# A graph-attention layer on one core: statistics of h from the gathered rows, three q tiles made ahead, weight loads behind the last k|v store, degrees kept in a table

## The chip, the core and the metric

The kernel runs on one core of one Trainium2 chip. The core has five engines, each with an in-order queue of its own: TensorE (PE, matrix products and transposes), VectorE (DVE), ScalarE (ACT), GpSimd (POOL), and SyncE (SP, which here only issues transfers). ACT and POOL issue transfers too. An instruction at the head of a queue that waits holds everything behind it in that queue.

The metric is the device time of one execution in microseconds, the median of several runs. Before the change it is 1834.15 us.

## The reference

A graph-transformer layer over 4096 nodes with 512 features. Source rows x and target rows h are normalized, q is made of h, and k and v of x, with 8 heads of 64. Each target node attends only to the nodes that its row of the 4096 x 4096 adjacency matrix names (about 17 of 4096, itself among them). Then come an output projection, a residual, a second normalization, a feed-forward net of 2048, two more residuals and a last normalization.

```python
hs = layer_norm(h_source, ln1_scale, ln1_bias)      # h_source is x
ht = layer_norm(h_target, ln1_scale, ln1_bias)
q = (ht @ Wq + bq).reshape(T, H, HD) / jnp.sqrt(jnp.float32(HD))
k = (hs @ Wk + bk).reshape(S, H, HD)
v = (hs @ Wv + bv).reshape(S, H, HD)
logits = jnp.einsum('thd,shd->hts', q, k)
logits = jnp.where(edge_mask[None] != 0, logits, NEG)
probs = jax.nn.softmax(logits, axis=-1)
ctx = jnp.einsum('hts,shd->thd', probs, v).reshape(T, D)
ht = ht + ctx @ Wo + bo
ht = layer_norm(ht, ln2_scale, ln2_bias)
out = ht + jax.nn.gelu(ht @ W1) @ W2
x = _layernorm(x + out)
```

## The kernel before

The kernel never forms the full logits. It reads the adjacency matrix once, turns each row into a short list of edges, and gathers the k|v rows that a list names.

**Stage 1: k|v rows and lists.** `project` takes x in 16 pairs of 128-row tiles: it measures each row (`measure`, with `stats`, L697 and L698), scales it on ACT (L890), transposes it on PE (L904), multiplies by Wk and Wv (L929, `source`), copies the products from PSUM (L931, ACT) and stores 128 rows of k|v in the DRAM table `kvd` (L935, issued by ACT). Beside it `edges(i)` reads the adjacency rows of tile i in four quarters of 512 KB (L713, issued by SP). ACT forms the signs of a quarter and counts them (L728), DVE weights them by position and finds the largest of five segments (L733, L735), and a decoding step at the end of a tile (L742 to L759) writes up to 24 column numbers into a record. What may be left over goes to `rest_d` (L766, issued by SP). The buffer is `ring`, 20 slots of 4 KB a partition: slots 0 to 7 hold quarters of the first NA + FILL tiles, 8 to 11 rows of h, 12 to 16 rows of x. Later quarters use two `wide` slots (17 and 18). Three sign buffers lie in slot 19. In the attention the slots 0 to 16, later 0 to 19, hold gathered k|v rows.

**Statistics of h.** In stage 1 the kernel also loads all 32 tiles of h in order of their rows (`ask`, L795) and measures them (`moments`, L805). At the end of the list stage it makes 1/sigma and -mean/sigma for all of them at once and writes both into the records (L1407 to L1411).

**The sort.** The records of 16 tiles are ordered by degree (`sort`): DVE counts, PE sums by matrix products (L838, L846), and POOL scatters 16 x 128 records to their places in DRAM (L853). After that, tile i of the attention holds nodes of like degree, and TILES gives each tile's largest degree, 11 to 39. The first half (NA = 16 tiles) is sorted in stage 1, the second half during the attention, after `other_lists`.

**The attention.** For a tile, `prefetch` loads its sorted records (L979), and `front` makes q in steps: gather rows of h by the TGT column (POOL), a small DVE step L994, normalization on ACT (L995), transposes (L999), the product with Wq (L1008) and the finish on DVE (L1013). L994 changes no value; it ties the record to the latest k|v copy or logits (`latest`), so that the front isn't issued too early. `issue` starts the gathers of k|v rows (L966, one per edge column), in groups of S = 3 columns. For a group, DVE forms the products with q (L1217) and the sums by head (L1222), ACT the exponentials, DVE and ACT the weighted v rows (L1181, L1201), and PE adds them up by transposing into PSUM (L1189). `finish` divides by the sum, projects (L1112), adds the residual, normalizes, and hands h2T to the FFN. `feed` runs the FFN of a group of tiles (L1325, L1328, L1334), and `end` the last normalization and the indirect store of the output. At the end `verdict` checks degrees and sums; the degrees come back from DRAM by two loads (L1259).

**What sets the order.** `_weave` runs generators as streams: each yields a cost, and the stream with the lowest total goes on. Streams of stage 1 are `projections`, `prepare` (lists of the first half, sort, first fronts) and `fill` (FILL more lists); of the second stage the attention, the FFN, `other_lists` and `weights`. That is the order in which instructions are written. A scheduler then moves them, engine by engine, by its own estimates, as far as dependences allow. The loads of the second half of W1 and W2 (`weights`, L586 and L587) are issued by ACT into memory that stage 1 gives back.

Of the kernel before, what the change touches and what calls it, by code (L numbers as in the profile page):

```python
# [377 lines left out]
DEG, TGT, ROW, RST, E0 = 0, 1, 2, 3, 5  # L378
# [65 lines left out]
def adj_resnorm_kernel(  # L444
# [88 lines left out]
    with tc.tile_pool(name="keep", bufs=1) as keep:  # L533
        ident = keep.tile([P, P], F32, name="ident")
        make_identity(nc, ident)
        mhalf = keep.tile([P, NT], F32, name="mhalf")
# [10 lines left out]
        degs = keep.tile([P, NT, 1], I32, name="degs")  # L547
# [3 lines left out]
        with ExitStack() as late:  # L551
# [57 lines left out]
            def list_constants():  # L609
# [17 lines left out]
                for R, (i0, n) in zip(Rs, PARTS):  # L627
                    nc.gpsimd.memset(R, 0)
                    for c, base in ((TGT, i0 * P), (ROW, 0)):
                        nc.gpsimd.iota(R[:, :, c], pattern=[[P, n]], base=base,  # L630
                                       channel_multiplier=1)
# [69 lines left out]
            held, moms = [], list(range(NT))  # L701
            mvh = wp.tile([P, NT, 2], F32, name="mvh")
# [3 lines left out]
            FILL = 5  # L706
# [9 lines left out]
            def edges(i):  # L716
# [4 lines left out]
                for h in range(NQ):  # L721
# [12 lines left out]
                    for s, (w0, w1) in enumerate(SEGS):  # L734
                        nc.vector.max(cand[:, h * SQ + s, :], wd[:, w0:w1])  # L735
                    if h == 1:
                        keep_rest()
                    if h % 2 and moms:
                        moments(moms.pop(0))
                    yield 2.0  # L740
# [20 lines left out]
                yield 4.0  # L761
# [29 lines left out]

            asked = list(range(NT))

            def ask(i):
                nc.sync.dma_start(hrow(i), h_target[i * P:(i + 1) * P, :])  # L795

            def hrow(i):
                return ring[:, DEEP + i // 2 % 4, i % 2 * D:(i % 2 + 1) * D]

            def moments(i):  # L800

                while asked and len(asked) > NT - 4 - i:
                    ask(asked.pop(0))
                t = hrow(i)
                stats(ip, t, mvh[:, i, :], "n0")  # L805

            def sort(part):
# [44 lines left out]
                for i in range(n):  # L852
# [7 lines left out]
                    yield 1.3  # L860
# [3 lines left out]
            def project(order, t=None):  # L864
# [54 lines left out]
                def source(n, j):  # L919
                    g, hT = order[n], state[n][1]  # L920
                    if asked or moms:
                        kvr = sp.tile([P, 2 * D], F32, name="tq", bufs=3)
                    else:

                        kvr = ring[:, 8 + (n * G + j) % 3, :]
# [6 lines left out]
                    if n >= 14:  # L932
                        latest[:] = [kvr[:, 0:1]]
                    r0 = 1 + (g * G + j) * P
                    nc.scalar.dma_start(kvd[r0:r0 + P, :], kvr)  # L935
# [27 lines left out]
            recs, tqs, h2Ts, done, ready, latest = {}, {}, {}, set(), [], []  # L963
# [187 lines left out]
            def first_fronts():  # L1151
# [6 lines left out]
                while not latest:  # L1158
                    yield None
# [326 lines left out]
```

## Time and profile before

| | us |
|---|---|
| median of 3 runs | 1834.15 |
| lowest and highest | 1833.16, 1836.34 |
| span of the profiled execution | 1826.4 |
| lists of the first half done, sort begins (L813) | 195.4 |
| scatter of the first sort, first and last | 240.8 to 261.5 |
| first gather of k|v rows issued | 301.6 |
| first value products on PE (L1189) | 320.1 |
| second sort begins (L813) | 591.5 |

The page cuts the span into 40 slices of 45.7 us. A digit is the busy share in tenths:

```profile
PE   7989983698998989999998998999999999999997
DVE  6999855999999838786967998999888797988200
ACT  5767634487987637676767777778777676787311
POOL 1000143746566477657567778877574656763101
PEclk9999996698999999999998999999999999999999
DMA  9999958988896648767769978787776767674000
```

Slices 1 to 6 are stage 1, 7 and 8 the passage to the attention, and the rest attention and FFN side by side. "PEclk" is the granted TensorE clock; it falls to about 0.7 in slices 7 and 8, where PE has little to do. In a group line the columns are: source line, engine and operation, output and input, shapes, count, then busy us and mean ns of one, then idle time of the engine just before. An idle time with an arrow names what ended it.

### The profile page before, as it was taken

The page shows a single profiled execution, that of the slowest core. Times are in us where ns is not written, and L with a number is a line of the kernel's source. Part 1 is how long each engine was busy: PE and PEld are TensorE (multiplying, and loading weights), DVE is VectorE, ACT ScalarE, POOL GpSimd, SP SyncE. Part 2 cuts the span into 40 slices and gives each one's busy share as a digit, 9 for nine tenths or more (in the row PEclk, how much of TensorE's full clock was granted, in tenths as well). Part 3 has the DMA queues.
Part 4 walks back from the last instruction along what each step waited for, and adds up shares of the span by engine and source line. Part 5 has one row for each costly group of instructions (what it writes and reads, how often), then busy time and mean ns, then how long its engine had stood idle before and what let it go on. Part 6 is the DMA issues. An engine that isn't in the chain of part 4 may idle for free. (4 is left out here: it accounts for less than half of the span.)

```text
span 1826.4 us, 22937 instructions
## 1 busy us (share of the span) xinstructions
PE 1687.8 (92%) x7030; PEld 1102.5 (60%) x7030; DVE 1432.2 (78%) x2628; ACT 1222.0 (67%) x3119; POOL 973.8 (53%) x834
## 2 busy tenths in 40 slices
PE   7989983698998989999998998999999999999997
PEld 3444431475666656767676666666666666667664
DVE  6999855999999838786967998999888797988200
ACT  5767634487987637676767777778777676787311
POOL 1000143746566477657567778877574656763101
PEclk9999996698999999999998999999999999999999
DMA  9999958988896648767769978787776767674000
GB/s 354 373 395 365 341 192 309 360 291 312 286 331 231 209 121 312 245 239 260 261 211 308 308 245 302 252 296 265 240 272 222 256 214 262 228 269 159 17 7 25
DMA packets 144396, 463.27 MB, mean 254 GB/s; under 512 B 20628, under 2 KB 25800, under 8 KB 144264
## 3 DMA queue, kind: packets, MB, share of 16 engines
q0 software_dynamic: 96656, 342.64, 54.7%
q1 hardware_dynamic: 39792, 96.00, 14.6%
q10 hardware_dynamic: 7816, 23.08, 3.3%
q8 instruction: 58, 0.95, 0.2%
q14 instruction: 74, 0.61, 0.1%
HBM read 430.76 MB, written 30.89 MB: 253 GB/s over the span
## 5 line engine op out<-in xcount | busy, mean ns | idle before, releaser
L966 POOL DMA_INDIRECT kv<-kvd,rec x603 | 751.4, 1246 | 376.2 <-PE cps L1189 161.4
L1334 PE MATMUL po<-w,gt 128*128 128x512 f32 x1024 | 464.9, 597 | 6.2 <-ACT gt L1328 6.0
L1325 PE MATMUL pf<-h2T,w 128*128 128x256 f32 (+1 forms) x2176 | 464.8, 367 | 0.3 <-ACT h2T L1143 0.3
L1325 PEld LDWEIGHTS pf<-h2T,w 128*128 128x128 f32 x2176 | 388.1, 190 | 64.6 <-issue 20.7
L1217 DVE TENSOR_TENSOR kv<-kv,tq 128x1536 f32<-128x1536 f32 (+2 forms) x211 | 351.7, 1675 | 88.1 <-DMA kv<-kvd,rec 82.9
L1201 ACT ACTIVATE kv<-kv,pa 128x64 f32<-128x64 f32 x1520 | 391.2, 336 | 4.4
L1222 DVE TENSOR_REDUCE lg<-kv 128x24 f32<-128x1536 f32 (+2 forms) x211 | 350.0, 1666 | 1.0 <-ACT pa L1198 0.2
L1189 PE MATMUL cps<-ident,kv 128*128 128x128 f32 x2008 | 269.0, 283 | 53.4 <-issue 23.5
L1189 PEld LDWEIGHTS cps<-ident,kv 128*128 128x128 f32 x2008 | 243.3, 147 | 122.4 <-issue 68.9
L1334 PEld LDWEIGHTS po<-w,gt 128*128 128x128 f32 x1024 | 188.6, 192 | 202.4 <-issue 195.5
L1181 DVE TENSOR_TENSOR kv<-kv,p 128x1024 f32<-128x1024 f32 (+1 forms) x211 | 250.9, 1193 | 23.8 <-ACT p L1226 20.3
L687 POOL TENSOR_TENSOR n_rs<-n_ve,mhalf 128x2 f32<-128x2 f32 (+2 forms) x51 | 46.4, 909 | 336.9 <-DVE n_ve L680 177.7
L728 ACT ACTIVATE kv<-kv 128x1024 uint8<-128x1024 int32 x128 | 134.8, 1054 | 77.1 <-DMA kv<-in_adj_dram 43.3
L1328 ACT ACTIVATE gt<-pf 128x512 f32<-128x512 f32 x128 | 76.3, 597 | 99.2 <-PE pf L1325 87.8
L1328 ACT ACT_TABLE_LOAD x103 | 132.1, 1283 | 1.6
L1008 PE MATMUL t<-wq,tq 128*128 128x512 f32 x256 | 122.2, 621 | 11.0 <-ACT tq L1002 7.8
L929 PE MATMUL pq<-wk,h2T 128*128 128x512 f32 x256 | 124.4, 630 | 7.2 <-ACT tq L931 3.6
L735 DVE MAX8 cand<-kv 128x8 uint16<-128x103 uint16 (+1 forms) x640 | 130.0, 252 | 0.5
L1226 ACT ACTIVATE p<-lg 128x24 f32<-128x24 f32 (+2 forms) x179 | 39.2, 219 | 128.8 <-DVE lg L1222 114.1
L1112 PE MATMUL t<-wo,rb 128*128 128x512 f32 x256 | 116.5, 597 | 0.0
L929 PE MATMUL pq<-wv,h2T 128*128 128x512 f32 x256 | 115.2, 593 | 0.8 <-ACT tq L931 0.8
L929 PEld LDWEIGHTS pq<-wk,h2T 128*128 128x128 f32 x256 | 50.3, 203 | 72.9 <-issue 59.1
(158 smaller groups left out, 1578.4 us busy)
## 6 DMA issues: line engine op xcount, KB each, us to landing
kv<-in_adj_dram SPq DMA_DIRECT2D x128, 512.0 KB
kvd<-tq ACTq DMA_DIRECT2D x24, 512.0 KB
kv<-kvd,rec POOLq DMA_INDIRECT x603
kv<-in_L_gnn_h_target_dram SPq DMA_DIRECT2D x32, 256.0 KB
kv<-in_x_dram SPq DMA_DIRECT2D x15, 512.0 KB
rest_d<-gid SPq DMA_DIRECT2D x32, 160.0 KB
w<-in_L_gnn_W_dram SPq DMA_DIRECT2D x4, 1024.0 KB
kvd<-kv ACTq DMA_DIRECT2D x8, 512.0 KB
```

The lines of the kernel that those rows point to most:

```text
L728: nc.scalar.activation(sg, a, AF.Sign, accum_out=dpart[:, i, h:h + 1])
L735: nc.vector.max(cand[:, h * SQ + s, :], wd[:, w0:w1])
L929: nc.tensor.matmul(pkv, hT[:, kc, j * P:(j + 1) * P], w[:, kc, :], start=kc == 0, stop=kc == KC - 1)
L966: nc.gpsimd.indirect_dma_start(out=dst, out_offset=None, in_=table[:, :], in_offset=bass.IndirectOffsetOnAxis(ap=idx, axis=0))
L1181: nc.vector.tensor_tensor(v4, v4, p[:, j0:j0 + m, :].unsqueeze(3) .to_broadcast([P, m, H, HD]), ALU.mult)
L1189: nc.tensor.matmul(cps[:, c, :], kv[:, j, D + c * P:D + (c + 1) * P], ident, is_transpose=True, start=j0 + j == 0 and c == 0, stop=j0 + n ...
L1201: nc.scalar.mul(v, v, pa[:, hd:hd + 1])
L1217: nc.vector.tensor_tensor(kv[:, :n, :D], kv[:, :n, :D], tq[:, :D].unsqueeze(1).to_broadcast([P, n, D]), ALU.mult)
L1222: nc.vector.tensor_reduce(lg[:, :n, :], kv[:, :n, :D].rearrange("p j (h d) -> p j h d", h=H), AX.X, ALU.add)
L1325: nc.tensor.matmul(pf[:, k, :], w1[(f0 + k) // KC][:, kc, (f0 + k) % KC * P:((f0 + k) % KC + 1) * P], h2T[:, kc, :w], start=kc == 0, stop= ...
L1328: nc.scalar.activation(gt, pf, AF.Gelu_apprx_tanh)
L1334: nc.tensor.matmul(po[j], gt[:, k, j * P:(j + 1) * P], w2[(f0 + k) // KC][:, (f0 + k) % KC, :], start=False, stop=f0 + k == FC - 1, skip_g ...
```

## The change

1. *Statistics of h.* `ask`, `hrow`, `moments` and the columns ROW and RST of the records are gone; a record has 26 words instead of 29. `front` measures the rows that it has gathered: `stats` and `shifted` on DVE, `power` on POOL, `negmean` on DVE, then ACT. A copy puts degree and target of the tile into a table `tags`, which output store, x gather and `verdict` read; the two loads L1259 are gone.
2. *Order.* `latest` and L994 are gone. `tc.issue_after(ins)` makes the instructions of its block, on the engine of `ins`, follow `ins` in that engine's order; it adds no semaphore. `newest` holds the last list or logits instruction on DVE and the last k|v store or scaled v row on ACT. The statistics and the normalization in `front`, and the loads in `weights`, stand behind those.
3. *q rows ahead.* EARLY is 3 instead of 2, and later fronts idle one step less.
4. *Buffers.* k|v rows before the store use ring slots 8 to 11 instead of three `tq` buffers; FILL is 6 instead of 5; records have 6 buffers instead of 7.
5. *Costs of the weave.* A list is charged 1.8 a quarter and 3.6 for decoding instead of 2.0 and 4.0; a scatter of the second sort 3.0 instead of 1.3.

```diff
-DEG, TGT, ROW, RST, E0 = 0, 1, 2, 3, 5
+DEG, TGT, E0 = 0, 1, 2
...
-        degs = keep.tile([P, NT, 1], I32, name="degs")
+        tags = keep.tile([P, NT, 2], I32, name="tags")
...
-            FILL = 5
+            FILL = 6
...
-                    if h % 2 and moms:
-                        moments(moms.pop(0))
-                    yield 2.0
+                    yield 1.8
...
-                yield 4.0
+                yield 3.6
...
-                    yield 1.3
+                    yield 3.0 if part else 1.3
...
-                    if asked or moms:
-                        kvr = sp.tile([P, 2 * D], F32, name="tq", bufs=3)
-                    else:
-
-                        kvr = ring[:, 8 + (n * G + j) % 3, :]
+                    kvr = ring[:, DEEP + (n * G + j) % 4, :]
...
-                    nc.scalar.dma_start(kvd[r0:r0 + P, :], kvr)
+                    newest["act"] = nc.scalar.dma_start(kvd[r0:r0 + P, :], kvr).ins
...
-                rec = sp.tile([P, E0 + MAXE], I32, name="rec", bufs=7)
+                rec = sp.tile([P, E0 + MAXE], I32, name="rec", bufs=6)
...
-                m = rec[:, RST:RST + 2].bitcast(F32)
-                nc.vector.scalar_tensor_tensor(m, m, latest[-1], m, op0=ALU.bypass, op1=ALU.max)
-                nc.scalar.activation(t, t, AF.Identity, bias=m[:, 1:2], scale=m[:, 0:1])
+                mv = sp.tile([P, 1, 2], F32, name="n0_mv")
+                with tc.issue_after(newest["dve"]):
+                    nc.vector.tensor_copy(tags[:, i, :], rec[:, DEG:TGT + 1])
+                    stats(sp, t, mv[:, 0, :], "n0")
+                    ve = shifted(sp, mv, 1, "n0")
+                yield
+                rs = power(sp, None, 1, "n0", ve)
+                yield
+                with tc.issue_after(newest["dve"]):
+                    nm = negmean(sp, mv, rs, 1, "n0")
+                with tc.issue_after(newest["act"]):
+                    nc.scalar.activation(t, t, AF.Identity, bias=nm, scale=rs)
                 yield
...
-            EARLY = 2
+            EARLY = 3
...
-                    fronts[i] = front(i, 2 * lead + (2 if i > NA else 0))
+                    fronts[i] = front(i, max(0, 2 * lead - 1) + (2 if i > NA else 0))
...
-                while not latest:
-                    yield None
...
-                for (i0, n), rec in zip(PARTS, recs_d):
-                    nc.sync.dma_start(degs[:, i0:i0 + n, :], rec.rearrange("(n p) w -> p n w", p=P)
-                                      [:, :, DEG:DEG + 1])
...
-                while moms:
-                    moments(moms.pop(0))
-                rs, nm = rstd_of(wp, mvh, NT, "n0")
-                for R, (i0, n) in zip(Rs, PARTS):
-                    Rf = R.bitcast(F32)
-                    nc.vector.tensor_copy(Rf[:, :, RST], rs[:, i0:i0 + n])
-                    nc.vector.tensor_copy(Rf[:, :, RST + 1], nm[:, i0:i0 + n])
...
-                    load_quarter(pool, q + 2, nc.scalar)
+                    with tc.issue_after(newest["act"]):
+                        load_quarter(pool, q + 2, nc.scalar)
```

## The prediction

> **What bounds the kernel now.** I read the page first (busy shares, the 40 slices), then the busy time by stretch, then the waits of the one stretch where TensorE (PE) idles, then the timelines of the five queues there. One execution spans 1826.4 us and the median is 1834.15, so 7.7 us lie around the span; I sum against the span and carry the difference over. The chain of waits covers only the last 3 us here and carries nothing. Columns of the stretches: length, busy us (x instructions) of PE, its weight loads, VectorE (DVE), ScalarE (ACT), GpSimd (POOL), then granted clock, DMA share, GB/s.
>
> ```profile
> PE 1687.8 (92%) x7030; PEld 1102.5 (60%) x7030; DVE 1432.2 (78%) x2628; ACT 1222.0 (67%) x3119; POOL 973.8 (53%) x834
> ...
> 0.00:225.00 225.00, 207.17 (x550) 96.67 (x551) 196.55 (x855) 153.95 (x283) 20.57 (x35) 0.98 0.98 366
> 225.00:297.00 72.00, 56.33 (x139) 25.88 (x138) 41.70 (x163) 31.99 (x63) 25.03 (x28) 0.88 0.63 212
> 297.00:320.00 23.00, 0.00 (x0) 0.00 (x0) 10.63 (x25) 7.98 (x20) 14.46 (x13) 0.60 1.00 387
> 320.00:591.00 271.00, 236.42 (x1111) 167.76 (x1112) 264.73 (x546) 208.53 (x548) 170.68 (x131) 0.91 0.84 301
> 591.00:1000.00 409.00, 390.87 (x1790) 272.19 (x1789) 305.32 (x321) 271.26 (x753) 264.67 (x232) 0.97 0.71 241
> 1000.00:1200.00 200.00, 187.88 (x841) 129.02 (x838) 181.07 (x190) 151.44 (x423) 161.19 (x119) 0.98 0.80 273
> ```
>
> PE is the bound over most of the span, so only PE's gaps can be won. To 225 us DMA (share 0.98), DVE (197 of 225) and PE (7.3 us per k|v tile without a gap) are level. From 225 to 320 the projections run out and attention isn't ready: PE works 56 of 95 us. From 320 to 591 DVE is full (265 of 271) and PE idles 35. After that PE is 94 to 97% full. The waits of the gap (engine, line, what it waited for, total, times, longest):
>
> ```profile
> POOL rec L853 <- DVE kv L850: 36.9, 1, 36.9
> POOL kv L966 <- DMA w<-in_L_gnn_W_dram: 24.0, 1, 24.0
> PE cps L1189 <- issue: 23.5, 1, 23.5
> DVE gid L747 <- DMA rest_d<-gid: 19.3, 2, 18.3
> ACT kv L728 <- DMA kv<-in_adj_dram: 16.9, 5, 5.5
> DVE kv L1217 <- DMA kv<-kvd,rec: 12.3, 1, 12.3
> ACT tq L995 <- DVE rec L994: 11.3, 1, 11.3
> ACT kv L931 <- DMA rec<-R,kv: 10.5, 1, 10.5
> ```
>
> They are one story, which SP's queue opens:
>
> ```profile
> 240.12 0.33 SPq L713 DMA_DIRECT2D kv<-in_adj_dram  x1
> 262.73 0.38 SPq L1259 DMA_DIRECT2D degs<-rec  x1
> 263.19 14.29 SPq L766 DMA_DIRECT2D rest_d<-gid  x2
> ```
>
> The read of the degrees (L1259) belongs to the end, but stands in SP's order right behind the first sort. It waits there for the 16 scatters (POOL, 240.8 to 261.5 us). Behind it SP holds the store of gid and all adj loads for 22 us. DVE therefore stops at L747 for 18.3 us, with L994 of the first two q tiles queued behind it; their L995 on ACT waits 11.3, and PE 7.4. ACT has meanwhile stood 10.5 us at the weight load placed among the last k|v copies. Then the first gather waits until 301.58: the last k|v store went out at 290.38, behind a weight load of 289.78, on DMA engines that are full to 320 (share 1.00).
>
> **What the Trainium skill says.** "DMA: Bandwidth & Descriptors", section Issuing engines are not separate DMA queues: DMAs of scalar, sync and gpsimd all run on the same 16 engines and interleave. The trace agrees: at 297 to 320 the gathers share 387 GB/s with weights and adj, and the first DVE instruction on them waits 12.3 us. "VectorE: DVE Perf Modes", section The TRN2 errata: SBUF operations pay a fixed cost per instruction. The trace agrees: a 128x2 operation here takes 0.16 to 0.22 us. "Perfetto Trace Analysis", Optimization Strategy: regimes with different limits can be interleaved; this trace has such regimes (DVE full 320 to 591, PE after).
>
> **The change part by part.**
>
> *Statistics out of stage 1.* Gone are 32 of 64 L697 (42.3 us for all) and 32 L698 (5.4), 26.6 us of DVE, and 32 loads of 256 KB, 8.4 MB, at 366 GB/s 23 us of DMA. Both were full, but so is PE: to 225 us it lost only about 16 us, 11 of them at the start. So I count no faster k|v tiles; the room is taken by lists. The weave charges 10.8 instead of 12 per list, and in the changed order ACT has 16.75 list tiles at k|v tile 20 (before 15.25) and 21.75 at tile 26 (before 19.75). Bytes agree: 18.5 lists read ahead against 17 is 3 MB more, h some 7 MB less.
>
> *The first sort.* In DVE's order it moves from 26 to 23 k|v tiles on PE: 3 x 7.3 = 22 us earlier, plus PE's 6.5 us stall at L846, which had list work before it. I take 206 us for the first scatter instead of 240.8. POOL's 16 scatters (1.26 us apart) end at 227, the record loads at 232, land near 235 (before: 6.9 us from issue to the first gather), gathers issue 235 to 239, land about 240 to 244.
>
> *New wait on DVE.* The copies to the table and the three statistics stand in DVE's order at list 21.2 to 21.5, reached at about 218. They wait for records (235) and gathers (240): some 20 us of DVE. Behind them are lists; ACT, only three sign buffers ahead, stops, and with it the copies of k|v tiles 27 and 28. PE has three PSUM buffers of cover and stalls about 10 us, where before it stalled 6.5 + 1.1 + 7.4 = 15. Bounds: 0 to 20.
>
> *End of the projections.* At 222 PE has 26 tiles; 6 x 7.3 = 44, plus 10, plus three fronts (12 transposes at 0.11, 12 matmuls at 0.43, 7 us) gives 283; before it was 296.6 with two. The degrees now come from a table, so SP is not held (-22 us on that queue). Weight loads stand behind the last store and ACT's first exponentials, so store and first gathers have no 4 MB beside them. Last store about 285, landed 289, first gathers in by 295. DVE must be at list 27 by then (it was 22.5): 5.5 lists from 245. A list costs 7.4 us of DVE when interleaved (196.6 busy to 225, less 64 statistics at 0.75 and 6 for the rest, over 19.5 lists) and 9.4 alone (four quarters at 1.29 plus 4.2 of decoding). At 8, 44 us: 289. From list 22 on quarters use only two wide buffers: 5.3 us each at 291 to 312 under full DMA. Without the weights I take 2.4, 20 quarters in 48 us. So first cps at 302 instead of 320: **-18 us**; bounds +15 (5.3 us each, partly) and -28 (no stall). The weights' 11 us of DMA (4 MB at 387 GB/s) now lie beside the first tiles; the FFN that needs them started at 374, the gathers have a 17-slot ring: nothing, at worst 5.
>
> *320 to 591, DVE full.* 4.5 lists were done earlier: -36 us of DVE. Each front adds L697 0.68, L698 0.17, shift 0.18, negated mean 0.16, and a copy taken as 0.15 (a 128x16 cast is 0.15): 1.34, or 0.96 with the overlap of neighbours; I take 1.15, less the removed L994 (0.21), 0.95. Waits per front: DVE for POOL's power 0.7 (L692 waited 11.9 us over 17 such hand-offs in attention), the gather 0.5 (ACT waited 15.3 over 30; the statistics now stand a step earlier, so 0.5 to 1). Nine fronts at 2.2 is 20. Net -16, of which PE, with 35 us idle, can take **-15** (bounds 0 and -25).
>
> *After 591.* Twenty fronts at 2.2 are 44 us of DVE, which idles 104 + 19 there to 1200 and 76 to 1700. In 1000 to 1200 DVE has 19 us left: five fronts, 11 us, half on the path: 5. The other fifteen, 33 us, I charge at a fifth: 6. **+11**, bounds 0 and +44. POOL gets 29 powers of 0.86 = 25 us and waits about 3 us for each (51.5 over 17), some 110 us; it loses the 24.5 us at which record loads waited for output stores. Behind a waiting power stand gathers; DVE waited only 70 us for gathers in attention, and POOL's own largest wait is for PE to free the ring (161 us), which is cover. Nothing, within the bound.
>
> *Rest.* Smaller records (26 words for 29), the smaller ring of records, and the end's table without two loads: no cost seen on the path, since the last stretch is PE's.
>
> Sum: -18 - 15 + 11 = -22. Span 1804, **median 1812 us**.
>
> **Rivals.**
> A, the forecast: 1812, own range 1797 to 1827.
> B, late costs hidden: DVE's waits after 591 fall wholly in its idle time and PE doesn't stall at the statistics: -28 - 15 = -43, 1791. For it: 199 us of idle DVE; against: every tile's chain passes DVE.
> C, the lists brought forward hold attention back: quarters at 4 us or more on two buffers, first cps at 320 or later; the lists come off later: 15 - 25 + 11 = +1, 1835. For it: 5.3 us measured; against: no weights beside them.
> D, slower: DVE's negated mean waits for POOL's power, the power stands behind gathers that wait for PE to free ring slots, and PE waits for DVE. At the longest such wait seen (5.5 us) plus 0.95, 29 fronts are 187 us of DVE; if a third reaches PE, +62 - 18 - 15 = +29: 1863. It decides from 2.5 us a front, where (2.5 + 0.95) x 29 / 3 = 33 eats both gains. For it: POOL waits 161 us for PE. Against: 0.7 us measured on the same hand-off.
> That the change doesn't do what it says is excluded by the order for the moved instructions.
>
> **How the numbers follow.** A 0.54, B 0.14, C 0.14, D 0.18. No change means within 0.2% (3.7 us), about what a measurement of this kernel can tell. Faster: A 0.52, B 0.14, C 0.06 = 0.72. Same: A 0.02, C 0.04 = 0.06. Slower: C 0.04, D 0.18 = 0.22. Range: 1788 to 1839; left out are the lower part of B (0.05) and most of D (0.14).
>
> **What would show it.** Right: no wait of SP at 240, first scatter near 206, a DVE wait on h gathers near 218 to 240, first cps near 302, PE idle of 320 to 591 falling from 35 to about 20, negated-mean waits under 1 us a front. Wrong: PE stalled over 20 us at the statistics, first cps not before 320, or DVE waits on POOL above 2.5 us a front.

## The result, and the profile after

The changed kernel takes 1898.56 us (median of four runs, 1892.78 to 1899.81) where the kernel before takes 1833.66 beside it: a ratio of 1.0352, 95% interval 1.0329 to 1.0376. It is 3.5% slower. The forecast was 1812. The profiled execution spans 1898.1 us, 71.7 more than before.

The busy time by stretch, columns as before:

```profile
0.00:225.00 225.00, 198.38 (x519) 92.19 (x520) 191.23 (x842) 157.30 (x289) 15.05 (x32) 0.96 0.96 350
225.00:297.00 72.00, 60.34 (x156) 28.23 (x155) 45.38 (x194) 38.19 (x75) 25.67 (x30) 0.91 0.52 166
297.00:320.00 23.00, 12.35 (x29) 5.13 (x27) 18.80 (x81) 10.65 (x19) 0.00 (x0) 0.87 0.75 238
320.00:591.00 271.00, 186.91 (x868) 134.77 (x869) 221.96 (x410) 154.65 (x446) 153.20 (x127) 0.81 0.76 269
591.00:1000.00 409.00, 391.57 (x1792) 271.05 (x1790) 297.08 (x346) 262.53 (x714) 284.52 (x238) 0.98 0.70 234
1000.00:1200.00 200.00, 187.02 (x838) 128.79 (x837) 174.22 (x181) 151.32 (x422) 150.93 (x118) 0.96 0.80 268
```

The loss lies ahead of 591 us. In 320 to 591 PE works 187 us (before 236), and DVE, which was full, works 222 (before 265). From 591 us on the rows are nearly those of before, only later. In 225 to 297 DMA falls to a share of 0.52 (before 0.63): its engines have room.

A better ruler than equal stretches is the moment at which the attention of a tile is finished (the product of cps and rb on DVE). The kernel before has it at 344 us for tile 1, 448 for tile 4, 628 for tile 8, 690 for tile 9, 1228 for tile 20 and 1717 for tile 32. The rows below say how much later a kernel reaches the same tile, in one profile each, and the ratio of its time to before.

```
run                      t1   t4   t8   t9  t20  t32   ratio (95% interval)
changed kernel          +34  +32  +66  +55  +62  +72   1.0352 (1.0329-1.0376)
stats_alone              -4   -7  -10  -12   -4   +6   1.0039 (1.0021-1.0057)
early_alone              -2   -4   +9   +5  +11  +12   1.0065 (1.0042-1.0089)
weights_alone            +9   +3   +9   +7  +15  +27   1.0094 (1.0074-1.0114)
pace_alone              +22  +17  +19   +3  +14  +14   1.0025 (1.0000-1.0051)
table_alone              +3   +4   +4   +4   +3   +8   1.0067 (1.0043-1.0091)
all_but_stats           +25  +13  +33  +23  +35  +34   (see there)
weights_unheld          +30  +29  +51  +38  +44  +52   1.0277 (1.0235-1.0320)
lists_slower             +9   +1  +21  +19  +29  +31   1.0189 (1.0143-1.0234)
after_early_old         +22  +15  +25   +8  +17  +18   1.0108 (1.0070-1.0146)
after_idle_old          +30  +15  +25   +8  +21  +22   1.0125 (1.0087-1.0163)
after_idle_longer       +32  +21  +25  +12  +30  +38   1.0196 (1.0161-1.0230)
stats_of_resident       +36  +27  +54  +41  +39  +46   1.0271 (1.0231-1.0311)
stats_no_power           -5   -9  -12  -13  -18  -13   0.9910 (0.9879-0.9942)
stats_mean_on_gpsimd     -4   -6   -5   -7   +5  +23   1.0130 (1.0096-1.0165)
stats_later_mean          0   -4   +7   -7  +13  +23   1.0109 (1.0073-1.0144)
power_on_vector          -4   -7   -1   -4   +1   +5   1.0020 (1.0003-1.0037)
power_on_vector_short    +4  +12  +31  +31  +40  +41   1.0180 (1.0149-1.0212)
half                     +7   +5  +12  +17  +50  +90   1.0469 (1.0435-1.0503)
```

So the changed kernel loses 34 us by its first tile, another 34 between tiles 4 and 8, wins 11 back at tile 9, and drifts by 17 after that. Late offsets of one profile are good to some 7 us: a profiled execution lies up to 6.7 us off its kernel's median (`weights_alone`). The ratios of the parts added one at a time (the rows `early_alone` to `table_alone`) don't add up to the whole.

The waits of the changed kernel from 225 to 340 us (engine, line, what it waited for, total, times, longest):

```profile
ACT kv L726 <- DMA kv<-in_adj_dram: 30.3, 14, 4.0
ACT kv L726 <- DVE cand L733: 20.8, 4, 13.0
...
DVE tags L970 <- DMA rec<-rec: 10.1, 2, 9.9
...
PE cps L1171 <- issue: 28.3, 1, 28.3
...
POOL kv L941 <- DMA kv<-in_adj_dram: 40.9, 1, 40.9
```

ACT stands 51 us at quarters of lists, 30.3 of them for data (before 16.9) and 20.8 for DVE, and POOL stands 40.9 us before its first gather (before 24.0). The last product of the projections on PE ends at 309.3 us (before 289.7). The last k|v store goes out at 313.6 us (before 290.4), the first gather at 320.9 (before 301.6), the first value products run at 337.7 (before 320.1).

### The profile page after: what moved, and what is told of

Same layout as the page of the kernel before. It is cut to its first block, busy times and chain, and to the rows that moved or that the text cites. A ratio compares the mean times of both kernels' runs of the same rounds, so it can differ in the third digit from the quotient of the medians.

```text
span 1898.1 us, 23012 instructions
## 1 busy us (share of the span) xinstructions
PE 1704.0 (90%) x7030; PEld 1108.9 (58%) x7030; DVE 1440.3 (76%) x2686; ACT 1225.3 (65%) x3117; POOL 1028.1 (54%) x863
## 3 DMA queue, kind: packets, MB, share of 16 engines
q1 hardware_dynamic: 31056, 87.59, 13.3%
## 5 line engine op out<-in xcount | busy, mean ns | idle before, releaser
L941 POOL DMA_INDIRECT kv<-kvd,rec x603 | 768.5, 1274 | 347.0 <-issue 120.2
L1303 PE MATMUL pf<-h2T,w 128*128 128x256 f32 (+1 forms) x2176 | 475.3, 372 | 5.6 <-issue 5.4
L1303 PEld LDWEIGHTS pf<-h2T,w 128*128 128x128 f32 x2176 | 393.4, 194 | 72.3 <-issue 27.0
L1199 DVE TENSOR_TENSOR kv<-kv,tq 128x1536 f32<-128x1536 f32 (+2 forms) x211 | 351.5, 1677 | 58.5 <-DMA kv<-kvd,rec 45.9
L686 POOL TENSOR_TENSOR n_rs<-n_ve,mhalf 128x2 f32<-128x2 f32 (+1 forms) x82 | 72.9, 889 | 380.2 <-DVE n_ve L679 182.4
L726 ACT ACTIVATE kv<-kv 128x1024 uint8<-128x1024 int32 x128 | 135.1, 1059 | 130.2 <-DVE cand L733 56.3
L906 PE MATMUL pq<-wv,h2T 128*128 128x512 f32 x256 | 124.4, 631 | 12.7 <-ACT kv L908 9.4
L992 PE MATMUL t<-wq,tq 128*128 128x512 f32 x256 | 120.6, 615 | 16.4 <-ACT tq L986 16.4
L733 DVE MAX8 cand<-kv 128x8 uint16<-128x103 uint16 (+1 forms) x640 | 132.3, 258 | 0.8
L906 PE MATMUL pq<-wk,h2T 128*128 128x512 f32 x256 | 119.2, 609 | 5.8 <-DMA wk<-in_L_gnn_Wk_dram 3.4
L906 PEld LDWEIGHTS pq<-wv,h2T 128*128 128x128 f32 x256 | 51.2, 203 | 80.0 <-issue 60.2
```

Source lines behind the costliest of these rows:

```text
L726: nc.scalar.activation(sg, a, AF.Sign, accum_out=dpart[:, i, h:h + 1])
L733: newest["dve"] = nc.vector.max(cand[:, h * SQ + s, :], wd[:, w0:w1]).ins
L906: nc.tensor.matmul(pkv, hT[:, kc, j * P:(j + 1) * P], w[:, kc, :], start=kc == 0, stop=kc == KC - 1)
L941: nc.gpsimd.indirect_dma_start(out=dst, out_offset=None, in_=table[:, :], in_offset=bass.IndirectOffsetOnAxis(ap=idx, axis=0))
L1199: nc.vector.tensor_tensor(kv[:, :n, :D], kv[:, :n, :D], tq[:, :D].unsqueeze(1).to_broadcast([P, n, D]), ALU.mult)
L1303: nc.tensor.matmul(pf[:, k, :], w1[(f0 + k) // KC][:, kc, (f0 + k) % KC * P:((f0 + k) % KC + 1) * P], h2T[:, kc, :w], start=kc == 0, stop= ...
```

## Experiments

**Statistics alone, and all but the statistics.** The first is the changed kernel with five edits taken back, the second the kernel before with the same five and the table of degrees:

```diff
-            FILL = 6
+            FILL = 5
-                    yield 1.8
+                    yield 2.0
-                yield 3.6
+                yield 4.0
-                    yield 3.0 if part else 1.3
+                    yield 1.3
-            EARLY = 3
+            EARLY = 2
-                    fronts[i] = front(i, max(0, 2 * lead - 1) + (2 if i > NA else 0))
+                    fronts[i] = front(i, 2 * lead + (2 if i > NA else 0))
-                    with tc.issue_after(newest["act"]):
-                        load_quarter(pool, q + 2, nc.scalar)
+                    load_quarter(pool, q + 2, nc.scalar)
```

> The changed kernel with the statistics of h in the fronts and the degrees in the table, but the paces of the lists, the two early q rows, the idle steps of a front and the place of the weight loads as before. Lists on DVE at the first attention step: 24 (before 22.5, after 27.0). Theory L (lists pulled ahead hold the first attention back, and most of the 65 us is from the opening): the opening is near that of before, first cps about 322, time 1835 to 1850. Theory F (the statistics in the fronts couple DVE to POOL's gathers and cost some 40 us after 448 us): 1870 to 1885, with the loss after 448 us still there. Theory W (late weights): no weights late, so some 16 us less than after at least, 1880.

> The kernel before with everything of the change except the statistics: degrees in a table, weights behind the last k|v store, three early q rows, shorter idle of the fronts, faster pace of the lists and six of them in the fill. Lists on DVE at the first attention step: 25. Theory L: the lists still come too early, loss of 20 to 30 us, 1855 to 1865. Theory W: the weights still lie beside the first gathers, at least +16, 1850. Theory F: what is lost is the opening alone, no further loss after 448 us, time at most 1870, and the sum of the two losses of this run and of the one with the statistics alone is about 65 us.

The statistics alone cost 0.4%, 7 us, as theory L expected. That kernel also keeps the change's buffers and `issue_after`, which weren't run apart. In the other kernel the degrees in the table are compared with the limits in another order of tiles, so that the program also runs its general path behind the layer (7817 us); its first 1848 us, the layer itself, are all that is used. There the tiles lose 25 us at the opening, another 20 between tiles 4 and 8, and 34 at the end, with the statistics still in stage 1. So most of the loss isn't the statistics by themselves, and theory F, in the form that they cost 40 us alone, fell.

**Two parts taken back, one at a time.** First the hold on the weight loads, then the pace of the lists (the first three pairs of lines above: the lists of the fill, the cost of a quarter and of a decoding).

> The changed kernel with the hold on the last weight loads taken away, so that they stand among the last k|v copies as before; nothing else edited. Lists on DVE at the first attention step fall from 27.0 to 25.75. Theory W: the 16 us between first cps and the end of the first tile come back, 1880 to 1885. Theory L: a stage earlier lists still stand before the last k|v store, so less than 8 us come back, above 1890. Theory F: the same as L, and the loss after 448 us unchanged.

> The changed kernel with the pace of the lists in the weave as before (five in the fill, costs 2.0 and 4.0); the rest of the change stays, weights held. Lists on DVE at the first attention step fall from 27.0 to 25.0, the first sort goes back to 27 k|v tiles. Theory L: the projections end earlier, first cps at 325 to 330 instead of 338, time 1880 or less. Theory W and theory F: the time stays at 1890 to 1900, since weights and fronts are as in the changed kernel.

Both win, by 0.75% (14 us, as theory W expected) and 1.6% (30 us, as theory L expected). Either alone leaves the loss of about 20 us between tiles 4 and 8.

**The parts added one at a time** to the kernel of the statistics alone, and the table added to the kernel before:

```diff
+                nc.vector.tensor_copy(degs[:, i, :], rec[:, DEG:DEG + 1])
...
-                for (i0, n), rec in zip(PARTS, recs_d):
-                    nc.sync.dma_start(degs[:, i0:i0 + n, :], rec.rearrange("(n p) w -> p n w", p=P)
-                                      [:, :, DEG:DEG + 1])
-                for i, cap in enumerate(CAPS_A + CAPS_B):
+                for i, (_, cap) in enumerate(TILES):
```

> The kernel of the statistics alone, with the pace of the lists put back (six in the fill, costs 1.8 and 3.6): lists stand at 25.75 at the first attention step, the first sort at 24 k|v tiles. Theory L: the last k|v store and first cps come 10 us or more later than with the statistics alone, 1865 to 1872. Theory W (the pace costs only together with late weights): 1840 to 1848.

> The kernel of the statistics alone, with the hold on the last weight loads put back. Theory W (4 MB of weights beside the first gathers cost by themselves): 1855, +16, with the loss between first cps and first tile. Theory L (the hold costs only because it lets lists pass: they stand at 25.0 at the first attention step instead of 23.75): first cps about 5 to 10 us later, and the rest beside the gathers under 8. Rival (without the lists it is hidden): 1840.

> The kernel of the statistics alone, with the three early q rows and the shorter idle of the fronts put back (weights, pace and sort as before). In all three runs with these two edits the tiles lost about 20 us between 448 and 628 us, and in the one without them nothing. Theory E (the early rows or the shorter idle make that loss): 1855 to 1862, with the 20 us between 448 and 628 us. Theory P (the pace of the second sort's scatters or the lists make it): 1836 to 1843, no loss there.

> The kernel before with one edit: the degrees are copied from each record into the table in the fronts, and SP's two reads of the degrees go. Prediction's step (SP not held for 22 us): SP's adj loads go out from 240 us on, VectorE's 18 us wait for gid goes, first cps 5 to 18 us earlier, 1816 to 1829. Rival (the scatters, record loads and the last k|v store set the first gather anyway): 1831, within 0.2% of before.

*Pace.* The first tile comes 22 us later than before and 26 later than with the statistics alone. 16 us come back at tile 9: DVE's last list step (L733) starts at 552 us instead of 580, the last scatter of the second sort comes at 631 instead of 653, and DVE's wait for k|v rows between tiles 8 and 9 falls from 10.9 us to none. At the end nothing is left of the loss (1.0025 against 1.0039), so theory L, which expected 1865 to 1872 us, missed.

Where the opening is lost is seen on ACT and PE. ACT's timeline of that kernel (start, duration, what it waited for; ACTq is its queue of transfers):

```profile
294.16 1.06 ACT L726 ACTIVATE kv<-kv 128x1024 uint8<-128x1024 int32 x1 [3.62 <-DMA kv<-in_adj_dram]
...
300.11 0.57 ACT L908 COPY kv<-pq 128x512 f32<-128x512 f32 x1
...
309.82 1.06 ACT L726 ACTIVATE kv<-kv 128x1024 uint8<-128x1024 int32 x1 [3.73 <-DMA kv<-in_adj_dram]
...
312.66 0.57 ACT L908 COPY kv<-pq 128x512 f32<-128x512 f32 x1
313.26 0.33 ACTq L910 DMA_DIRECT2D kvd<-kv  x1
```

PE's with the pace, then with the statistics alone:

```profile
282.51 1.97 PE L983 MATMUL t<-ident,tq 128*128 128x128 f32 x8 [7.22 <-ACT tq L979]
...
287.67 7.03 PE L992 MATMUL t<-wq,tq 128*128 128x512 f32 x16
294.54 3.60 PE L906 MATMUL pq<-wk,h2T 128*128 128x512 f32 x8
...
304.84 3.60 PE L906 MATMUL pq<-wv,h2T 128*128 128x512 f32 x8
```

```profile
277.06 3.60 PE L906 MATMUL pq<-wv,h2T 128*128 128x512 f32 x8
283.69 1.97 PE L983 MATMUL t<-ident,tq 128*128 128x128 f32 x8 [3.04 <-ACT tq L979]
292.17 9.35 PE L992 MATMUL t<-wq,tq 128*128 128x512 f32 x16 [6.50 <-ACT tq L986]
```

Between the last copies of k|v products (L908) stand signs of list quarters (L726) that wait for their data: two wide buffers, and a new load can only start when one is free. From 270 to 325 us ACT waits 26.8 us for such quarters here, 11.0 with the statistics alone. In ACT's order 25.25 lists stand ahead of the last store here, 23.75 in that one, 26.0 in the changed kernel, 22.0 before.

But that the last copies wait there isn't what delays the last store by 22.7 us (313.3 against 290.6): it goes out 4.9 us behind PE's last k|v product here, 9.9 us behind it with the statistics alone. PE itself ends 27.7 us later, at 308.4 instead of 280.7. With the new pace the transposes and q products of the first fronts (L983, L992) stand in PE's order ahead of the last two k|v tiles, 9.0 us of work, and behind all of them with the statistics alone. And from 200 us to that product PE waits 13.3 us for ACT, against 2.6. In the changed kernel three fronts stand there, 13.0 us of work. With the lists' old pace and the rest of the change (`lists_slower`) none does, and PE ends at 285.0. So the pace is shown to cost the opening, through PE's order and PE's waits for ACT, which make 20 of the 27.7 us; the other 8 are spread.

*Weights held.* It costs 0.55%, 10 us, and 13 us at the first tile. The busy time from 320 to 400 us with the weights held, then with the statistics alone:

```profile
320.00:400.00 80.00, 52.14 (x281) 40.66 (x282) 73.00 (x123) 43.65 (x137) 53.02 (x45) 0.81 0.95 362
```

```profile
320.00:400.00 80.00, 61.15 (x341) 46.33 (x340) 76.00 (x115) 50.19 (x154) 57.94 (x48) 0.87 0.88 311
```

51 GB/s more on engines that are busy to 0.95, and PE 9 us less. The weights go out at 317 to 330 us instead of 262 to 292, and the gathers of the first tiles share the engines with 4 MB. A part of the 13 us is lost before that: 24.5 lists instead of 23.75 stand ahead of the last store, which goes out 3.8 us later (294.4). Theory L expected this.

*Early rows and shorter idle.* 0.26%, 5 us, with 16 us lost between tiles 4 and 8 against the statistics alone, which are partly won back later. So theory E had the place and not the time, 1855 to 1862. At the first tile the parts do add up: -4 for the statistics, 26 for the pace, 13 for the weights and 2 for these make 37, and the changed kernel is 34 late.

*The table.* The kernel before with this one edit is 0.67% slower, where both theories expected it faster or level. SP no longer stands 22 us at the reads of the degrees, but DVE now waits in the fronts where it waited for gid. Waits of that kernel, 225 to 325 us:

```profile
DVE degs L993 <- DMA rec<-rec: 17.4, 4, 15.1
...
DVE gid L747 <- DMA rest_d<-gid: 0.3, 1, 0.3
```

The wait for gid was 19.3 us. It went, and 17.4 us of waiting for records took its place: the copy is the first thing on DVE that needs the loaded record. SP, free of the reads, stood 25.5 us at its stores of gid instead, for DVE (from 254 us; before 14.3).

**The idle of the fronts.** The changed kernel, first with the old number of early rows and the old idle, then with the old idle only, then one step longer than the old one (2 lead + 1):

> The changed kernel with two early q rows and the old idle of the fronts; pace, held weights and statistics stay as changed. The pace alone cost nothing in the end (0.3%, since the tiles won 16 us back between 628 and 690 us), the held weights 0.5% and the early rows 0.3% on top of the statistics alone, but together they cost 3.5%. Theory X (the early rows or the shorter idle keep the tiles from winning back what the pace lost at the opening): 1850 to 1860, with the win between 628 and 690 back. Rival Y (pace and held weights together make it, the early rows are by the way): 1885 or more.

> The changed kernel with three early q rows, but the old idle of the fronts. Theory X1 (the shorter idle is what hurts: a front's statistics stand closer behind the gather of their rows): 1850 to 1865. Theory X2 (the third early row, which moves every later step, is what hurts): 1890 to 1900.

> The changed kernel with the idle of a front one step longer than before the change (2 lead + 1, where the change has 2 lead - 1). Theory F: the statistics stand still farther behind the gather, the same as with the old idle or better, 1840 to 1855. Theory O (the front's later steps must not come too late for their tile): slower than with the old idle, 1860 or more. Chance (any other order is quicker than the changed one): anything from 1845 to 1870.

Old idle alone takes 1.0352 down to 1.0125: one step, some 41 us, as theory X1 expected. The third early row costs nothing that these runs tell (1.0108 and 1.0125). The longer idle is slower again, 1.0196, as theory O expected: the old value lies between two worse ones. With the old idle the tiles win back 17 us from tile 8 to tile 9, as with the pace alone.

How much the shorter idle costs depends on the pace. With the weights held the time is 1.0094 with neither (`weights_alone`), 1.0108 with the pace (`after_early_old`), 1.0189 with the shorter idle and the third row (`lists_slower`), and 1.0352 with all: 3 us, 17 us, and 47 together. The last three also charge 3.0 for a scatter of the second sort; that charge was never run alone.

What the missing step does is seen in the changed kernel's timelines between 500 and 550 us. GpSimd's:

```profile
500.84 4.12 POOL L1280 DMA_INDIRECT out_dram<-xt,tags  x1 [0.30 <-issue]
509.32 1.71 POOL L941 DMA_INDIRECT xt<-in_x_dram,tags  x1 [4.36 <-DMA out_dram<-xt,tags]
...
515.11 0.96 POOL L941 DMA_INDIRECT tq<-in_L_gnn_h_target_dram,rec  x1 [0.31 <-issue]
524.01 1.40 POOL L686 TENSOR_TENSOR n_rs<-n_ve,mhalf 128x1 f32<-128x1 f32 x1 [7.94 <-DVE n_ve L679]
525.60 0.98 POOL L941 DMA_INDIRECT kv<-kvd,rec  x1 [0.19 <-issue]
```

VectorE's:

```profile
520.18 0.70 DVE L696 BATCH_NORM_STATS2 n_st<-tq 128x6 f32<-128x512 f32 x1 [7.67 <-DMA tq<-in_L_gnn_h_target_dram,rec]
...
537.54 1.76 DVE L1199 TENSOR_TENSOR kv<-kv,tq 128x1536 f32<-128x1536 f32 x1 [6.04 <-issue]
```

ScalarE's and TensorE's:

```profile
541.60 0.22 ACT L1207 ACTIVATE p<-lg 128x24 f32<-128x24 f32 x1 [5.53 <-DVE lg L1203]
...
549.32 1.49 ACT L986 ACTIVATE tq<-t,b1r,cols 128x128 f32<-128x128 f32 x4
```

```profile
549.81 5.16 PE L992 MATMUL t<-wq,tq 128*128 128x512 f32 x8 [8.21 <-ACT tq L986]
```

To be read in a circle. The gather of h stands on POOL behind a gather of x that waits for an output store to land, so it goes out at 515.11. DVE is already at the statistics of that row and waits 7.67 us. The power of the same row stands at the head of POOL's queue and waits 7.94 us for DVE; behind it stand the k|v gathers. These go out from 525.60 on, and DVE waits 6.04 us before its next product with k|v rows. The profile names no releaser there ("issue"), but counted in order, the three columns of that product are the gathers of 512.60, 513.86 and 525.60. ACT then waits 5.53 us for the logits, and PE 8.21 for a copy that stands behind them on ACT. So one late row is passed on through all four engines.

From 340 to 640 us DVE waits 11.2 us for rows of h here and 2.9 with the old idle; POOL waits at the fronts' power 22.1 us here and 2.0 there. But in `after_early_old` POOL waits 19.9 us there at a ratio of 1.0108, so the length of this wait alone isn't the price.

**Statistics over a resident tile** takes the first link away, with an unchanged order of instructions:

```diff
-                    stats(sp, t, mv[:, 0, :], "n0")
-                    ve = shifted(sp, mv, 1, "n0")
+                    stats(sp, bqr, mv[:, 0, :], "n0")
+                    ve = sp.tile([P, 1], F32, name="n0_ve")
+                    nc.vector.tensor_scalar(ve, mv[:, :, 1], 0.0, 1.0, op0=ALU.mult, op1=ALU.add)
```

> The changed kernel, with the statistics of the fronts taken over a tile that is always in SBUF (bqr) instead of the gathered row, and the variance replaced by 1 before the power: the same instructions in the same order on every engine, but VectorE need not wait for the gather of h; the rows are then scaled by 1 and hardly shifted, so the normalization of h is left out. Theory F (the shorter idle puts the statistics so close behind the gather that VectorE waits for it, and each such wait is passed on to the queue behind): 1855 to 1875, most of the 46 us that the idle costs. Theory O (the shorter idle costs through the places of the later steps, the transposes and the product of q, whatever VectorE waits for): 1885 to 1898.

1.0352 falls to 1.0271, some 15 us (6 to 23 by the two intervals): a part of what the idle costs, not most of it. DVE's waits for rows of h are gone, but from 320 us on it still waits 49.2 us for gathers of k|v rows, as in the changed kernel (45.9), where the old idle has 27.3. So the rest shows as late k|v rows; which of the moved steps makes them late wasn't told apart.

**The late loss of the statistics.** Alone they are 12 us ahead at tile 9 and 6 late at the end. First the power left out, then the negated mean a step later, then the mean's product on GpSimd (and its negation with the statistics), all in the kernel of the statistics alone:

```diff
-                rs = power(sp, None, 1, "n0", ve)
+                rs = ve
```

> The kernel of the statistics alone with GpSimd's power in the fronts left out (the variance itself is taken as the scale), so that VectorE's negated mean need not wait for GpSimd; the rows are then scaled wrongly. The statistics alone were 10 us ahead of before at 628 us and 6 us late at the end. Theory H (the hand-off of the power, some 10 us of VectorE's waits between 960 and 1180 us, makes the loss after 628 us): 1823 to 1830, at most 0.2% below before. Rival (the added VectorE work makes it): 1836 to 1842, no change.

> The kernel of the statistics alone with one more step between GpSimd's power and VectorE's negated mean, in the fronts. Theory H: VectorE's wait for the power shrinks, 1828 to 1836, if the front still ends in time. Rival (a longer front comes late for its tile, TensorE waits at the first product): 1840 to 1850.

```diff
-                with tc.issue_after(newest["dve"]):
-                    nm = negmean(sp, mv, rs, 1, "n0")
+                nm = sp.tile([P, 1], F32, name="n0_nm")
+                nc.gpsimd.tensor_tensor(nm, mv[:, :, 0], rs, ALU.mult)
```

> The kernel of the statistics alone, with the product of mean and power moved from VectorE to GpSimd (the mean is negated by VectorE right behind the statistics, so that VectorE waits for nothing of GpSimd in a front; ScalarE's normalization waits for GpSimd instead). Leaving the power out won 25 us, all between 960 and 1311 us. Theory H1 (what costs is that VectorE stands still for the hand-off): most of that comes back, 1818 to 1826, under before. Theory H2 (what costs is that the normalized row comes late, whichever engine waits): 1833 to 1842, as with the statistics alone.

Without the power the time is 0.9910 of before, 1.3% or 24 us less than with it, and below what theory H expected. In the profiles it is level with the statistics alone at 961 us and 19 ahead at 1311, and stays so. In this stretch DVE works 319 of 351 us, with the power 301; the rows with the power, then without:

```profile
960.00:1311.00 351.00, 324.24 (x1378) 215.70 (x1377) 300.90 (x333) 252.16 (x694) 256.14 (x203) 0.96 0.76 257
```

```profile
960.00:1311.00 351.00, 334.13 (x1464) 226.72 (x1463) 318.62 (x359) 269.78 (x741) 260.03 (x206) 0.98 0.81 272
```

But moving DVE's wait off DVE made the kernel slower. With the mean a step later it takes 1.0109, as the rival expected, though DVE's wait for the fronts' power from 960 to 1311 us falls from 8.6 us to 1.0. With the mean on GpSimd it takes 1.0130. Waits from 960 to 1311 us, of the statistics alone and then with the mean on GpSimd:

```profile
DVE n_nm L691 <- POOL n_rs L686: 18.5, 8, 4.3
```

```profile
ACT tq L980 <- POOL n_nm L977: 18.0, 6, 6.2
```

The first line serves the second normalization too: 8.6 of its 18.5 us belong to fronts (128x1). These went (7.0 us are left, all of the second normalization), and ACT waits 18.0 us at its normalization in their place, where it waited 8.5 for DVE's mean. So H1 fell. H2, that the row is late whoever waits, is left over and not shown; its 1833 to 1842 us were missed too, with 1851. A rival stands beside it: without the power POOL also loses 32 instructions that could hold k|v gathers behind them.

**The power on VectorE**, in eight instructions (a guess from the bits, two Newton steps), then the same with one step less in the front:

```diff
+                    nc.vector.tensor_single_scalar(rs.bitcast(I32), ve.bitcast(I32), 1, op=ALU.logical_shift_right)
+                    nc.vector.tensor_scalar(rs.bitcast(I32), rs.bitcast(I32), -1.0, 1597463007.0, op0=ALU.mult, op1=ALU.add)
+                    for _ in range(2):
+                        nc.vector.scalar_tensor_tensor(nm, rs, -0.5, rs, op0=ALU.mult, op1=ALU.mult)
+                        nc.vector.tensor_mul(nm, nm, ve)
+                        nc.vector.scalar_tensor_tensor(rs, nm, 1.5, rs, op0=ALU.add, op1=ALU.mult)
-                rs = power(sp, None, 1, "n0", ve)
```

> The kernel of the statistics alone with the power of the fronts worked out by VectorE itself: a shift and a subtraction for a first guess and two steps of Newton's method, eight small instructions right behind the statistics in place of GpSimd's one; nothing is handed over. Leaving the power out gave 1814. Theory H2 (a row that is late by the hand-off to GpSimd is what costs): eight instructions of some 0.16 us, 1.3 us a front and 41 us of VectorE in all, of which it idles as much, so 1816 to 1828, under before. Rival (the added VectorE work eats the gain where VectorE is nearly full): 1832 to 1845.

> The same with one step less in the front, since the mean needs no step of its own any more. Theory H2: the row is ready a step earlier, the same as the other or up to 8 us less, 1812 to 1828. Theory O (places of the later steps matter whichever way they are moved, and the lists stand 0.5 later at the first attention step): 1832 to 1850.

1.0020: not told apart from the statistics alone (1.0039), whose interval it overlaps. H2 expected 1816 to 1828; the rival, that the added DVE work eats the gain, expected 1832 to 1845, and 1834 came. The eight cost 38 us of DVE over 32 fronts (six of 153 ns and two of 142 in each) and save a hand-off; the gain of 24 us isn't reached. One step less makes it 1.0180, 29 us more and slower than both theories expected: the second place where a front shortened by one step costs tens of microseconds.

**Half.** Statistics in the fronts for the first 16 tiles only, and a ring of six records instead of seven, for want of space.

> The kernel before with the statistics of h in the fronts for the first 16 tiles alone; for the other 16 they are taken ahead of the sort and lie in the records, as before. Weights, degrees, early rows, idle and pace as before. With the statistics alone the tiles were 10 us ahead at 628 us and 4 to 6 us late from 1310 us on. If the waits of VectorE for GpSimd's power after 1000 us made that late loss, this keeps some 5 to 10 us: 1823 to 1830, under before. Rival (the late loss is chance, or the gain at the opening came from all 32 rows): 1831 to 1840.

Slowest of all, outside both expectations, and inconclusive on its question: it is 23 us late at tile 16, and 67 more are lost after it, where its fronts work as before. There DVE waits 85.1 us for PE's q products (before 27.3) and 37.9 us for record loads (900 to 1720 us). In this kernel a record must live until its tile's output store, since the store takes its rows from it; that the missing seventh buffer is the cause is argued, not shown, and the larger wait for PE isn't explained by it here. No kernel with the whole computation was faster than before.

## Why the prediction was wrong

1. *Opening, -18.* Measured: first value products +17.6, at 337.7. The step that failed is the end of the projections on PE, "gives 283", on which "last store about 285" rests. PE ended at 309.3, and the store went out at 313.6. Three terms were wrong. At 222 us PE had 24 of the 32 tiles and not 26 (before 25.7): 15 us. Three fronts took 13.0 us ahead of the last tiles and not 7, since their q products are 24 of 0.43 us and not 12. PE's waits for ACT from 222 us on were 11.7 and not 10. These make 23 of the 26 us. I had counted the lists brought forward as DVE time only; the pace alone, 22 us late at the first tile, shows that they also hold ACT and let the fronts pass the last k|v tiles on PE. From the last store to the first value products it then took 24.1 us, less than the 29.7 before. "SP is not held" is true and worth nothing, as the table alone shows; the wait moved to the record, which I had counted, but beside a gain that wasn't there. The new wait on DVE came as forecast in kind: 12.8 us for records and rows of h, where I expected 20.
2. *"First scatter 206."* It came at 227.2. The first scan of the sort moved from 232.9 to 213.5 us on DVE, but PE's stall at the sort, counted as won, stayed (6.9 us, before 6.5), and from first scan to index the sort then took 13 us instead of 7.5, with a list's decoding in between.
3. *Weights, "nothing, at worst 5".* The hold costs 10 by itself, a part of it through the lists that it lets pass. The cover I named, a ring of 17 slots, is empty when the first tile begins: its gathers are on the path. I had read that gathers, weights and adj share 387 GB/s at 297 to 320 us, and didn't apply it to this place.
4. *320 to 591, -15.* From tile 1 to tile 8 the changed kernel lost 32 us, and PE idled 84 us in 320 to 591 where I expected 20. The step that failed is the gather wait of a front, "0.5 to 1" us because "the statistics now stand a step earlier". Direct waits for rows of h were 11.2 us from 340 to 640, in three places, not far above my sum for nine fronts. But each is handed on through POOL's queue, and the step saved, which I priced in this wait alone, cost 41 us altogether, some 15 of it through this wait. I priced each wait by its length and not by what stood queued behind it on the other side of the hand-off; that gathers stand behind a waiting power on POOL I had named, and put at nothing. The 36 us of DVE work done early did come off, but as idle time of DVE (busy 222 of 271 us). DVE's own wait for the power stayed under 1 us a front, as forecast.
5. *After 591, +11.* The changed kernel loses 6 us from tile 8 to tile 32, the statistics alone 16 (of which 5 to 10 may be chance). The sum for this stretch came out near, but by luck: it charged DVE's added work and direct waits. Without the power this loss is gone though the statistics stay, and leaving it out is worth 24 us. How the power costs that is open.
6. *Rivals.* C had the cause of the opening (the lists brought forward, first cps at 320 or later), though not PE's order, but let the lists' return pay for it, as with the pace alone; with the shorter idle this payment stayed away. D had the power as a cost; its price in the statistics alone is 24 us, below D's point of decision, and not as a long wait of DVE. Neither reached 1898, because the parts don't add: one at a time they cost 7, 5, 10 and nothing (22 of 64), and the pace and the shorter idle cost most together (3, 17 and 47 us above).

What stays open: which of the steps moved by the shorter idle costs the other 26 us, why the order is so sharply best at the old value, and by which way the power costs 24 us.

## What to carry to other kernels

Work brought forward must be counted on every queue that it passes, above all on those that also carry the last steps of the stage before; here it was ACT's copies and PE's products, not DVE's time. A wait between two in-order engines that feed each other can cost what is queued behind it on both, so the place of a step may matter more than its duration: look at the engine that issues the data before a consumer is moved nearer to its gather. Change one such constant at a time: of this change the early row was nearly free, the pace was free alone and cost 30 us beside the shorter idle, and one step of idle was two thirds of the loss.

## What the runs showed that was not expected

A single step of delay in a generator, with no instruction added or removed, moved the time by 41 us and by 29 us in two kernels. With the lists' faster pace the products of the first fronts passed the last k|v tiles in TensorE's order. A power of 128x1 on GpSimd is short (0.77 us on average in the statistics alone), yet leaving 32 of them out won 24 us. A 128x1 instruction of VectorE takes 0.14 to 0.15 us whether it multiplies floats or shifts integers.
